# A four-layer graph network on one core: layer 3's product before its aggregation, and all engines reordered

## The chip, the cores and the metric

The kernel runs on one core of a Trainium2 chip. The metric is the device time of one execution in microseconds (us). The kernel before took 2079.52 us, the median of three runs between 2079.24 and 2079.53.

A core has five engines that run their own instruction streams in order and wait for one another by semaphores: TensorE (PE, matrix products into PSUM), VectorE (DVE), ScalarE (ACT), GpSimd (POOL) and SyncE (SP). In this kernel SP issues every DMA.

## The reference

`x` is 128 graphs of 128 nodes by 512 features, `adj` one 128 x 128 matrix of weights shared by all graphs. Four layers follow, each of the form `x = layernorm(x + layer(x))`:

```python
# layer 0: normalized adjacency
nadj = adj * deg**-0.5[:, None] * deg**-0.5[None, :]
y0 = nadj @ (x @ W0) + bias
# layer 1: with W1 = W2 = adj its result is one number per node, the same in all 512 features
# layer 2: attention without softmax
q, k, v = x @ Wq.T, x @ Wk.T, x @ Wv.T
rel = adj.T * (q @ k.T);  rel = rel / norm(rel, axis=2)
y2 = rel @ v
# layer 3: graph attention
h = x @ W
e = leaky_relu((h @ a1)[:, None] + (h @ a2)[None, :]) * adj
y3 = elu(softmax(e) @ h + beta * h)
```

The layernorm behind layer 1 takes its constant away again, so layers 0 and 1 share one layernorm with a changed variance (line 638). The kernel computes layer 3 as elu of (att + beta I) applied to x and W, in one order or the other. It leaves out the -1 of elu, a constant that the layernorm behind it takes away; elu + 1 is max(z, 0) + min(exp(z), 1).

## The kernel before

The 128 graphs are worked in 32 groups of four. All arithmetic is in float32. Each group goes through four large products, named for their weights: **w** (layer 0), **z** (x times Wq^T Wk, made in the head), **v** (layer 2's values) and **k** (layer 3's W). Each is made with one level of Strassen's scheme: seven block products in the order 1, 2, 5, 7, 6, 3, 4 instead of eight, with sums of blocks of the left side (four per group, tile S) and sums of blocks of the weights (made once). A block product is four matmul calls, each of which shows as two instructions in the profile. Product 6 is added in PSUM onto 1's bank, 3 onto 5's and 4 onto 7's.

Nothing is scheduled automatically. The order of the work is written out as a list of steps, `group.step`, in three strings: HEAD, then TURN once for each group from FIRST to the end less LAST (with group numbers shifted by one each time), then TAIL. Each engine's own order follows from this list. The head in the kernel before fills the pipeline with groups 0 to 3 and part of 4; TURN is repeated 21 times. The steps, with their engines:

- `ld`: SP loads x of a group (five tiles of x exist). `y`: PE makes (nadj x)^T, sixteen matmul calls of 128 x 128; `cy`: ACT copies it out; `sy`: POOL makes the sums S.
- `w1` to `w7`: the block products of w. `dw`: DVE adds them onto x; `tw`: ACT copies the 1+6 sum, `uw`: POOL adds that. `bi`: POOL adds the bias.
- `st`, `va`, `po`, `nb`, `ap` with w, v or k: layernorm. DVE takes statistics of each of the four graphs and the variance, POOL its power -1/2, DVE the shift, ACT applies both.
- `xt0` to `xt3`: DVE transposes x in squares of 32 into a tile u, of which there is one; `xd`: SP moves the squares with sixteen DMAs to their places, which completes the transpose; `sx`: POOL makes S.
- `z1` to `z7`, with `cz`, `dz`, `tz`, `uz`: z and its elimination into C_z by ACT, DVE and POOL. `r0` to `r3`: PE multiplies C_z with x transposed, 32 instructions. `rm`: DVE masks; `sq`: ACT takes norms; `rp`: POOL; `rt`: DVE transposes rel in squares; `wr`, `cr`: SP sends it through a DRAM tile and reads it back with four DMAs (`across`).
- `v1` to `v7`, with `cv`, `dv`, `tv`, `uv`: v into C_v. `f0` to `f3`: PE multiplies rel with C_v, one matmul call per graph; `fa`: DVE adds it, times the norm, onto x. 
- `sc`: DVE makes the two scores of each graph for layer 3; `pw`, `pe`: SP sends one through DRAM to all partitions. `pl`, `ej`, `ei`, `ex`, `rd`, `so`: leaky relu, mask, softmax and + beta I on ACT and DVE. `at`, `aw`, `cat`: att is transposed and moved as rel is.
- `h`: PE makes (att x)^T, sixteen matmul calls of 128 x 128 (pv in the profile); `ch`: ACT copies it out; `sh`: DVE makes S out of PSUM. `k1` to `k7`, with `ck`, `dk`, `tk`, `uk`: k into C_k. `ee`, `em`, `ea`: elu out of C_k, in three instructions a block: exp on ACT, max with 0 added onto x on DVE, min with 1 added onto x on DVE. `stk` to `apk`: the last layernorm; `fin`: SP stores a graph.

Line 552 holds the block products, 605 the matmuls of y and h, 691 rel's, 734 f's. Lines 441, 444 and 438 are the helpers of DVE, POOL and ACT. Lines 832, 836 and 840 are elu; 515 is the move of the transposed squares; 525 and 529 are the way through DRAM. Six banks of PSUM rotate among all matmul outputs; two more are held by the score vectors.

In a repeated round of the kernel before PE does w (of one group), h, v, f, k, y, z and r, the last two for the same group and next to each other.

Of the kernel before, what the change touches and what calls it, by code (L numbers as in the profile page):

```python
# [37 lines left out]
F32 = mybir.dt.float32  # L39
# [7 lines left out]
GB = 4  # L47
# [3 lines left out]
FIRST = 4  # L51
LAST = -7
# [4 lines left out]
0.dw7 0.bi00 0.w3 0.tw 0.bi11 1.ld 0.w4 0.bi01 0.uw10 0.dw3 1.y10 0.uw01 1.y00 0.dw4 1.cy10  # L57
1.y11 1.cy00 0.uw11 0.stw0 1.y01 1.cy11 0.stw1 1.sy1 s.g0 1.cy01 0.stw2 1.sy0 0.stw3 0.vaw s.q00
0.pow s.q01 s.g1 s.cg0 0.nbw 1.sy2 0.apw0 0.apw1 0.xt0 1.bi10 2.ld 3.ld 0.apw2 0.xt1 4.ld 1.sy3
0.apw3 0.xt2 s.g2 s.cg1 0.xt3 1.bi00 s.q02 s.q03 s.g3 s.q10 s.cg2 s.q11 s.q12 s.q13 s.bi 1.bi11  # L60
1.w1 0.xd s.cg3 s.s30 s.sg0 1.w2 1.dw1 1.bi01 s.sg2 1.w5 s.sg1 s.sg3 1.w7 1.dw5 1.dw2 s.s32 1.w6
1.dw7 s.s31 1.w3 1.tw s.s33 1.uw01 1.w4 1.uw10 1.dw3 1.stw0 s.t0 1.uw11 s.t1 1.dw4 s.ct0 s.t2
s.ct1 1.stw1 0.sx0 s.t3 s.ct2 0.z1 1.stw2 s.ct3 0.sx1 1.stw3 0.z2 0.cz1 1.vaw 0.sx2 s.sv0 1.pow
0.z5 0.dz2 0.sx3 1.nbw 1.apw0 0.z7 s.sv2 0.cz5 s.sv1 1.apw1 0.z6 0.dz7 1.apw2 1.xt0 1.apw3 s.sv3
0.z3 0.tz 1.xt1 0.uz11 1.xt2 1.xt3 0.z4 0.dz3 1.xd 2.y10 0.dz4 2.y00 2.cy10 2.bi10 2.y11 2.cy00
2.bi00 2.y01 2.cy11 2.sy0 0.r0 2.cy01 0.r1 2.sy1 0.r2 2.sy2 0.r3 0.v1 0.rm 2.bi11 0.rt 0.sq0
0.sq1 2.sy3 0.v2 0.cv1 0.wr 0.sq2 2.bi01 0.sq3 0.v5 0.dv2 0.rp 0.cr 1.sx0 0.v7 0.cv5 1.sx1 0.v6
0.dv7 1.sx2 0.v3 0.tv 1.sx3 0.uv11 0.v4 0.dv3 s.wa 0.dv4 0.f0 0.f1 0.fa0 0.stv0 0.f2 0.fa1 0.f3
0.fa2 3.y10 0.fa3 3.y00 3.cy10 3.bi10 0.stv1 3.y11 3.cy00 0.stv2 3.bi00 3.y01 3.cy11 0.stv3
3.sy0 1.z1 3.cy01 0.vav 0.pov 1.z2 1.cz1 3.sy1 0.nbv 0.apv0 0.apv1 1.z5 0.sc00 3.sy2 0.apv2  # L70
0.sc01 3.bi11 0.apv3 0.sc10 1.z7 1.cz5 0.sc11 3.sy3 0.sc20 1.z6 1.dz7 3.bi01 0.sc21 1.z3 1.tz
0.sc30 1.uz11 0.sc31 1.dz2 1.z4 0.pw 1.dz3 2.w1 1.dz4 2.w2 2.dw1 0.pe 2.w5 2.dw2 2.w7 2.dw5
0.pl0 0.pl1 0.pl2 0.pl3 2.w6 2.dw7 0.ej 0.ei 2.w3 2.tw 0.ex0 2.uw01 0.ex1 2.w4 0.ex2 2.uw10
2.dw3 0.ex3 2.stw0 2.uw11 1.r0 0.rd 2.dw4 1.r1 0.so0 0.so1 1.r2 0.so2 0.so3 2.stw1 1.r3 0.at
1.v1 1.rm 0.aw 2.stw2 1.sq0 1.v2 1.sq1 2.stw3 1.cv1 1.sq2 2.vaw 2.pow 1.sq3 1.v5 1.dv2 0.cat
1.rp 1.rt 2.nbw 2.apw0 1.v7 1.cv5 2.xt0 1.wr 2.apw1 1.v6 1.dv7 2.apw2 2.xt1 2.apw3 2.xt2 1.v3
1.tv 2.xt3 1.cr 1.uv11 1.v4 1.dv3 0.h10 2.xd 1.dv4 0.h00 0.ch10 0.h11 0.ch00 0.sh1 0.h01 0.ch11
0.sh0 1.f0 0.ch01 0.sh2 1.f1 1.fa0 1.f2 0.sh3 1.f3 1.fa1 1.fa2 0.k1 1.fa3 1.stv0 0.k2 0.ck1
1.stv1 1.stv2 0.k5 1.stv3 0.dk2 0.k7 0.ck5 1.vav 0.em00 1.pov 0.ee00 0.ea00 0.k6 0.dk7 2.sx0
1.nbv 1.apv0 2.sx1 0.k3 1.apv1 1.sc00 1.apv2 2.sx2 1.sc01 0.k4 1.apv3 1.sc10 2.sx3 0.tk 1.sc11  # L80
2.z1 1.sc20 0.uk11 1.sc21 1.sc30 0.ee11 2.z2 2.cz1 1.sc31 0.dk3 1.pw 2.z5 2.dz2 0.dk4 2.z7
0.em11 2.cz5 0.em01 0.ea11 2.z6 1.pe 2.dz7 0.ee01 0.em10 2.z3 0.ea01 2.tz 0.stk0 0.ee10 2.uz11
0.stk1 1.pl0 2.z4 1.pl1 2.dz3 1.pl2 1.pl3 0.ea10 2.r0 2.dz4 2.r1 1.ej 2.r2 0.stk2 1.ei 2.r3
0.stk3 1.ex0 2.v1 1.ex1 2.rm 1.ex2 0.vak 2.rt 0.pok 1.ex3 2.v2 2.cv1 2.wr 1.rd 1.so0 2.sq0 1.so1
1.so2 2.sq1 2.v5 1.so3 2.sq2 2.dv2 2.sq3 0.nbk 2.rp 0.apk0 2.v7 2.cr 1.at 2.cv5 0.apk1 2.v6
0.apk2 2.dv7 0.apk3 1.aw 0.fin0 2.v3 2.tv 0.fin1 2.uv11 0.fin2 2.v4 2.dv3 0.fin3 1.cat 2.f0
2.dv4 2.f1 2.fa0 2.stv0 2.f2 5.ld 2.fa1 2.f3 2.fa2 3.w1 2.fa3 2.stv1 3.w2 3.dw1 2.stv2 3.w5
3.dw2 2.stv3 3.w7 2.vav 3.dw5 2.pov 2.nbv 2.apv0 3.w6 3.dw7 2.apv1 2.sc00 2.apv2 2.sc01 3.w3
3.tw 2.sc10 2.apv3 3.uw01 2.sc11 3.w4 2.sc20 3.uw10 3.dw3 1.h10 2.sc21 3.uw11 1.h00 3.dw4 1.ch10
3.stw0 1.h11 1.ch00 3.stw1 1.h01 1.ch11 1.sh1 1.k1 1.ch01 1.sh0 1.sh2 1.k2 1.ck1 3.stw2 1.sh3  # L90
3.stw3 1.k5 2.sc30 3.vaw 2.sc31 1.k7 3.pow 1.ck5 1.dk2 2.pw 3.nbw 1.ee00 1.em00 1.k6 3.apw0
1.dk7 3.apw1 1.ea00 1.k3 3.xt0 3.apw2 3.xt1 3.apw3 2.pe 3.xt2 1.k4 1.tk 3.xt3 1.uk11 1.dk3 3.xd
4.y10 1.dk4 1.ee01 1.em11 4.y00 2.pl0 4.cy10 1.em01 4.y11 4.cy00 1.em10 2.pl1 4.y01 1.ea01
4.cy11 4.sy1 4.w1 1.stk0 2.pl2 4.cy01 1.stk1 2.pl3 4.sy0 1.ee11 4.w2 4.dw1 2.ej 1.ea11 4.w5 2.ei
4.sy2 1.ee10 4.dw2 2.ex0 4.bi10 4.w7 2.ex1 4.dw5 2.ex2 2.ex3 1.ea10 4.w6 4.dw7 4.sy3 2.rd 1.stk2
4.bi00 4.w3 4.tw 2.so0 2.so1 4.w4 2.so2 2.so3 1.stk3 3.sx0 2.at 3.z1 3.sx1 1.vak 2.aw 4.dw3
4.dw4 3.sx2 3.z2 3.cz1 1.pok 3.z5 3.dz2 2.cat 3.sx3 1.nbk 1.apk0 4.bi11 3.z7 3.cz5 1.apk1 1.fin0
4.bi01 1.apk2 1.fin1 3.z6 3.dz7 1.apk3 1.fin2 4.uw10 1.fin3 3.z3 4.uw01 4.uw11 4.stw0 3.z4
4.stw1 6.ld 3.tz 4.stw2 2.h10 3.uz11 3.dz3 2.h00 2.ch10 3.dz4 2.h11 2.ch00 4.stw3 2.h01 2.ch11
2.sh1 3.r0 4.vaw 2.ch01 2.sh0 4.pow 3.r1 2.sh2 4.nbw 3.r2 2.sh3 4.apw0 3.r3 4.apw1 4.xt0 4.apw2  # L100
3.v1 4.xt1 3.rm 4.apw3 4.xt2 3.sq0 3.v2 3.cv1 3.rt 3.sq1 4.xt3 3.wr 3.sq2 3.v5 3.sq3 3.dv2 3.rp
3.v7 3.cv5 3.cr 3.v6 3.dv7 3.v3 3.tv 3.uv11 3.v4 3.dv3 3.f0 4.xd 3.dv4 3.f1 3.fa0 3.stv0 3.f2
3.fa1 3.f3 3.fa2 2.k1 3.fa3 3.stv1 2.k2 2.ck1 3.stv2 3.stv3 2.k5 2.dk2 3.vav 2.ee00 2.em00 3.pov
2.k7 2.ck5 2.ea00 3.nbv 3.apv0 2.k6 2.dk7 3.apv1 3.sc00 3.apv2 3.sc01 2.k3 3.apv3 3.sc10 4.sx0
2.tk 3.sc11 2.k4 4.sx1 3.sc20 3.sc21 4.sx2 5.y10 3.sc30 5.y00 5.cy10 3.sc31 2.uk11 2.dk3 5.y11
3.pw 5.cy00 4.sx3 2.dk4 2.ee11 5.y01 5.cy11 2.em11
"""
TURN = """
4.z1 5.cy01 2.em01 2.em10 4.z2 4.cz1 3.pe 2.ea11 5.sy0 2.ee01 4.z5 4.dz2 5.sy1 4.z7 4.cz5 2.ea01
3.pl0 5.sy2 2.stk0 2.ee10 2.stk1 4.z6 3.pl1 5.bi10 3.pl2 4.dz7 3.pl3 3.ej 4.z3 4.tz 2.ea10 3.ei  # L110
4.uz11 4.z4 4.dz3 3.ex0 5.sy3 3.ex1 2.stk2 3.ex2 4.r0 2.stk3 3.ex3 5.bi00 4.dz4 4.r1 3.rd 5.bi11
2.vak 4.r2 4.r3 3.so0 2.pok 3.so1 5.w1 3.so2 3.so3 4.rm 5.bi01 3.at 4.sq0 5.w2 4.sq1 5.dw1 3.aw
4.sq2 2.nbk 4.sq3 2.apk0 5.w5 4.rp 5.dw2 2.apk1 2.fin0 2.apk2 2.fin1 4.rt 5.w7 2.apk3 3.cat
5.dw5 5.w6 5.dw7 4.wr 5.w3 5.tw 2.fin2 5.uw01 2.fin3 5.w4 5.uw10 5.dw3 4.cr 5.stw0 5.uw11 3.h10
5.dw4 3.h00 5.stw1 3.ch10 3.h11 5.stw2 3.ch00 7.ld 3.h01 5.stw3 3.ch11 3.sh0 4.v1 3.ch01 5.vaw
3.sh1 5.pow 3.sh2 4.v2 4.cv1 5.nbw 3.sh3 5.apw0 5.apw1 5.xt0 4.v5 4.dv2 5.apw2 5.xt1 5.apw3 4.v7
5.xt2 4.cv5 5.xt3 4.v6 4.dv7 4.v3 4.tv 4.uv11 4.v4 4.dv3 4.f0 5.xd 4.dv4 4.f1 4.fa0 4.stv0 4.f2
4.fa1 4.f3 4.fa2 3.k1 4.fa3 4.stv1 3.k2 3.ck1 4.stv2 4.stv3 3.k5 3.dk2 4.vav 3.ee00 3.em00 4.pov
3.k7 3.ck5 3.ea00 4.nbv 4.apv0 3.k6 3.dk7 4.apv1 4.sc00 4.apv2 4.sc01 3.k3 4.apv3 4.sc10 5.sx0
3.tk 4.sc11 3.k4 5.sx1 4.sc20 4.sc21 5.sx2 6.y10 4.sc30 6.y00 6.cy10 4.sc31 3.uk11 3.dk3 6.y11  # L120
4.pw 6.cy00 5.sx3 3.dk4 3.ee11 6.y01 6.cy11 3.em11
"""
TAIL = """
4.z1 5.cy01 2.em01 2.em10 4.z2 4.cz1 3.pe 2.ea11 5.sy0 2.ee01 4.z5 4.dz2 5.sy1 4.z7 4.cz5 2.ea01
3.pl0 5.sy2 2.stk0 2.ee10 2.stk1 4.z6 3.pl1 5.bi10 3.pl2 4.dz7 3.pl3 3.ej 4.z3 4.tz 2.ea10 3.ei
4.uz11 4.z4 4.dz3 3.ex0 5.sy3 3.ex1 2.stk2 3.ex2 4.r0 2.stk3 3.ex3 5.bi00 4.dz4 4.r1 3.rd 5.bi11
2.vak 4.r2 4.r3 3.so0 2.pok 3.so1 5.w1 3.so2 3.so3 4.rm 5.bi01 3.at 4.sq0 5.w2 4.sq1 5.dw1 3.aw
4.sq2 2.nbk 4.sq3 2.apk0 5.w5 4.rp 5.dw2 2.apk1 2.fin0 2.apk2 2.fin1 4.rt 5.w7 2.apk3 3.cat
5.dw5 5.w6 5.dw7 4.wr 5.w3 5.tw 2.fin2 5.uw01 2.fin3 5.w4 5.uw10 5.dw3 4.cr 5.stw0 5.uw11 3.h10
5.dw4 3.h00 5.stw1 3.ch10 3.h11 5.stw2 3.ch00 8.ld 3.h01 5.stw3 3.ch11 3.sh0 4.v1 3.ch01 5.vaw  # L130
3.sh1 5.pow 3.sh2 4.v2 4.cv1 5.nbw 3.sh3 5.apw0 5.apw1 5.xt0 4.v5 4.dv2 5.apw2 5.xt1 5.apw3 4.v7
5.xt2 4.cv5 5.xt3 4.v6 4.dv7 4.v3 4.tv 4.uv11 4.v4 4.dv3 4.f0 5.xd 4.dv4 4.f1 4.fa0 4.stv0 4.f2
4.fa1 4.f3 4.fa2 3.k1 4.fa3 4.stv1 3.k2 3.ck1 4.stv2 4.stv3 3.k5 3.dk2 4.vav 3.ee00 3.em00 4.pov
3.k7 3.ck5 3.ea00 4.nbv 4.apv0 3.k6 3.dk7 4.apv1 4.sc00 4.apv2 4.sc01 3.k3 4.apv3 4.sc10 5.sx0
# [788 lines left out]
```

## Time and profile before

| | before |
|---|---|
| median of three runs | 2079.52 us |
| the profiled execution, its own time | 2078.88 us |
| its span, first to last instruction | 2076.9 us |
| mean granted PE clock | 0.997 |
| DMA packets; of these under 512 B | 364,341; 283,425 |
| one move of transposed squares: 16 issues on SP | 11.54 us |
| relT's and attT's DMAs, 64 KB each, to landing | 2.0 us |
| elu's two DVE passes, mean | 1093 and 1155 ns |
| fa, DVE with one input from PSUM, mean | 697 ns |

The span and the run's time differ by what lies around the first and the last instruction, here 1.98 us. Means come from the groups of instructions by line; the mean of fa is its busy time, 89.2 us, over 128 instructions, since successive instructions overlap a little and the page's mean of one, 739 ns, counts the overlap twice. For PE this matters more: a block matmul shows 379 ns from start to modelled end, but 56 of them take 12.09 us, 216 ns each, since they are pipelined.

A row of waits reads: the waiting engine and what it ran next, what it waited for, the sum in us, how often, the longest. A row of the stretch table reads: the stretch, its length, then the busy time of PE, PE's weight load, DVE, ACT and POOL, the granted PE clock, the DMA share and GB/s.

### The profile page before, as it was taken

The numbers are of one execution on the slowest core, as the hardware profiler recorded it, in microseconds if no ns is written. First come the engines' busy times: TensorE is split into PE (matmuls) and PEld (weight loads), VectorE is DVE, ScalarE is ACT, GpSimd is POOL, SyncE is SP. The second block draws the span as 40 slices with busy tenths as digits, with TensorE's granted clock in tenths as the row PEclk, the third lists the DMA queues.
The fourth block names the chain that finished last, engine by engine and source line by source line (L and its number), as shares of the span: only waits on it lengthen the run. The fifth ranks groups of instructions, "written<-read, shape, count | busy, mean of one in ns | idle before, by whom it ended". The sixth has DMA issues, their size and how long they took to land.

```text
span 2076.9 us, 29797 instructions
## 1 busy us (share of the span) xinstructions
PE 2033.5 (98%) x10554; PEld 1796.7 (87%) x10554; DVE 1605.9 (77%) x3048; ACT 842.0 (41%) x1737; POOL 916.6 (44%) x712
## 2 busy tenths in 40 slices
PE   9999999999999999999999999999999999999996
PEld 6888988888888888888888888888888888888885
DVE  6578788777887778787778877788877878776777
ACT  2333434444443334343343443444343434343345
POOL 5632554434544445443355444454434554436211
PEclk9999999999999999999999999999999999999998
DMA  7222322332223332223322133222233122232212
GB/s 232 39 46 66 91 67 43 86 82 79 74 42 71 82 87 67 62 51 87 82 73 73 36 85 82 80 73 45 68 82 87 66 66 47 77 92 46 47 51 91
DMA packets 364341, 150.74 MB, mean 73 GB/s; under 512 B 283425, under 2 KB 316321, under 8 KB 364193
## 3 DMA queue, kind: packets, MB, share of 16 engines
q1 hardware_dynamic: 364192, 148.84, 28.3%
q8 instruction: 84, 1.38, 0.3%
q14 instruction: 65, 0.52, 0.1%
HBM read 64.82 MB, written 50.40 MB: 55 GB/s over the span
## 4 chain that ended last, share of the span: by engine, by line
PE 78%; DVE 16%; issue 4%; ACT 1%; SPq 1%; POOL 0%; DMA 0%; POOLq 0%; ACTq 0%; DVEq 0%
PE p_v L552 18%; PE p_w L552 18%; PE p_k L552 17%; PE pv L605 5%; PE p_z L552 5%; PE pf L734 5%; DVE x L840 4%; PE pr L691 4%; PE py L605 4%; DVE st_k L631 3%; DVE x L836 3%; DVE C_z L441 2%; DVE C_k L441 1%; ACT ex L832 1%; DVE nmax L790 1%
## 5 line engine op out<-in xcount | busy, mean ns | idle before, releaser
L441 DVE TENSOR_TENSOR x<-p_w,x 128x512 f32<-128x512 f32 x192 | 131.8, 688 | 153.6 <-PE p_w L552 77.7
L444 POOL TENSOR_TENSOR x<-x,t_w 128x512 f32<-128x512 f32 x96 | 119.3, 1271 | 173.2 <-ACT t_w L438 172.8
L753 DVE SCALAR_TENSOR_TENSOR prod<-x,wa_bc 128x512 f32<-128x512 f32 x256 | 175.7, 686 | 22.3 <-ACT x L653 8.7
L444 POOL TENSOR_TENSOR x<-x,bias_bc 128x512 f32<-128x512 f32 x128 | 173.0, 1363 | 14.1 <-PE py L605 13.1
L552 PE MATMUL p_k<-w_t,S_v 128*128 128x256 f32 x768 | 171.2, 379 | 1.6 <-ACT C_k L438 1.6
L552 PE MATMUL p_z<-S_x,gq_t 128*128 128x256 f32 x768 | 171.0, 379 | 0.0
L552 PE MATMUL p_v<-wvT_t,S_x 128*128 128x256 f32 x768 | 171.0, 379 | 0.0
L552 PE MATMUL p_w<-w_t,S_y 128*128 128x256 f32 x768 | 171.0, 379 | 0.0
L448 POOL TENSOR_TENSOR r_v<-v,minus_half 128x4 f32<-128x4 f32 x32 | 43.7, 1366 | 286.8 <-DVE v L640 286.6
L552 PEld LDWEIGHTS p_k<-w_t,S_v 128*128 128x128 f32 x768 | 145.8, 190 | 21.8 <-ACT C_k L438 2.0
L552 PEld LDWEIGHTS p_w<-w_t,S_y 128*128 128x128 f32 x768 | 145.9, 190 | 19.8
L552 PEld LDWEIGHTS p_v<-wvT_t,S_x 128*128 128x128 f32 x768 | 145.9, 190 | 19.8
L552 PEld LDWEIGHTS p_z<-S_x,gq_t 128*128 128x128 f32 x768 | 145.9, 190 | 19.8
L840 DVE SCALAR_TENSOR_TENSOR x<-ex,x 128x512 f32<-128x512 f32 x128 | 147.8, 1155 | 10.1 <-ACT ex L832 5.1
L832 ACT ACTIVATE ex<-C_k 128x512 f32<-128x512 f32 x128 | 80.8, 631 | 147.7 <-DVE x L840 84.4
L836 DVE SCALAR_TENSOR_TENSOR x<-C_k,x 128x512 f32<-128x512 f32 x128 | 135.6, 1093 | 0.0
L441 DVE TENSOR_TENSOR C_v<-p_v,t_v 128x512 f32<-128x512 f32 x64 | 44.3, 692 | 114.0 <-PE p_v L552 114.0
L444 POOL TENSOR_TENSOR C_v<-C_v,t_v 128x512 f32<-128x512 f32 x32 | 40.5, 1265 | 200.9 <-ACT t_v L438 196.0
L438 ACT COPY C_k<-p_k 128x512 f32<-128x512 f32 x64 | 37.2, 585 | 224.1 <-PE p_k L552 224.0
L605 PEld LDWEIGHTS py<-nadjT,x 128*128 128x128 f32 x1024 | 121.9, 196 | 2.7 <-DVE nadjT L372 0.8
L605 PE MATMUL py<-nadjT,x 128*128 128x128 f32 x1024 | 122.3, 279 | 0.4 <-DVE nadjT L372 0.4
L653 ACT ACTIVATE x<-x,nb,r_v 128x512 f32<-128x512 f32 x128 | 94.4, 804 | 68.3 <-DVE nb L647 68.3
(959 smaller groups left out, 4754.8 us busy)
## 6 DMA issues: line engine op xcount, KB each, us to landing
out_dram<-x SPq DMA_DIRECT2D x128, 256.0 KB, 2.3
x<-in_x_dram SPq DMA_DIRECT2D x31, 1024.0 KB, 5.4
d_r<-ru SPq DMA_DIRECT2D x32, 256.0 KB, 2.1
relT<-d_r SPq DMA_DIRECT2D x128, 64.0 KB, 2.0
s<-d_s SPq DMA_DIRECT2D x32, 256.0 KB, 3.9
d_a<-au SPq DMA_DIRECT2D x32, 256.0 KB, 2.0
attT<-d_a SPq DMA_DIRECT2D x128, 64.0 KB, 2.0
x<-in_x_dram SPq DMA_DIRECT2D x2, 512.0 KB, 4.6
```

What stands on the lines that cost most here:

```text
L441: nc.vector.tensor_tensor(o, a, b, f)
L444: nc.gpsimd.tensor_tensor(o, a, b, f)
L552: nc.tensor.matmul(ps[:, j, :], lhsT=lhsT, rhs=rhs, start=(i not in ONTO and j == 0 and kc == 0), stop=(j == 1 and kc == 1), skip_group_ch ...
L605: nc.tensor.matmul(o, lhsT=self.x_chunk(b, kc), rhs=rhs, start=True, stop=True)
L631: nc.vector.bn_stats(st, self.x[:, b, :])
L653: nc.scalar.activation(xt, xt, AF.Identity, bias=self.nb[k][:, b : b + 1], scale=self.rstd[k][:, b : b + 1],)
L691: nc.tensor.matmul(self.pr[:, b, :], lhsT=self.whole["z"][:, fc, b // 2, bass.ts(b % 2, P)], rhs=self.xT.chunk(b, fc), start=(fc == 0), st ...
L734: nc.tensor.matmul(self.pf[b], lhsT=self.relT.rearrange("p q r b -> p b (q r)")[:, b], rhs=self.whole["v"][:, b, :], start=True, stop=True,)
L753: nc.vector.scalar_tensor_tensor(prod, self.x[:, b, :], 1.0, wide(wa_bc[k]), ALU.mult, ALU.mult, accum_out=self.s[:, k, b : b + 1],)
L832: nc.scalar.activation(self.ex[p, h], self.k_block(p, h), AF.Exp)
L836: nc.vector.scalar_tensor_tensor(o, self.k_block(p, h), 0.0, o, ALU.max, ALU.add)
L840: nc.vector.scalar_tensor_tensor(o, self.ex[p, h], 1.0, o, ALU.min, ALU.add)
```

## The change

Layer 3 is turned around. The product with W is made first, out of x transposed, as z and v are; then att + beta I multiplies C_k, one matmul call per graph, as f does with C_v. elu reads its argument from PSUM, and exp writes its result back over it. The steps `h` (16 calls), `ch` and `sh` go. New are `nt` and `nd`, which transpose and move x after the second layernorm as `xt` and `xd` do after the first, through the same tile u, and `sn`, the sums of n on POOL. The x that is transposed there is the one that `sc` reads.

```diff
-                "k": Product(f"k_{g}", self.v, "3"),
+                "k": Product(f"k_{g}", self.nT, "3"),
...
-        def pe_h(self, p, h):
-            self.v.make(p, h, lambda o, b, kc: self.times(o, b, kc, self.attT[:, :, b, :]))
+        def nt(self, b):
+            self.nT.square(b, self.x[:, b, :])
+
+        def nd(self):
+            self.nT.move()
...
+        def left_times(self, k, left, b):
+            ps = psum.tile([P, D], F32, tag="bank", name=f"pl_{k}_{self.g}_{b}")
+            nc.tensor.matmul(ps, lhsT=left[:, b, :], rhs=self.whole[k][:, b, :], start=True, stop=True)
+            return ps
...
-        def ee(self, p, h):
-            self.ex[p, h] = mid.tile([P, 2, HD], F32, tag="ex", name=f"ex_{self.g}_{p}_{h}")
-            nc.scalar.activation(self.ex[p, h], self.k_block(p, h), AF.Exp)
-
-        def em(self, p, h):
-            o = self.x_block(p, h)
-            nc.vector.scalar_tensor_tensor(o, self.k_block(p, h), 0.0, o, ALU.max, ALU.add)
-
-        def ea(self, p, h):
-            o = self.x_block(p, h)
-            nc.vector.scalar_tensor_tensor(o, self.ex[p, h], 1.0, o, ALU.min, ALU.add)
+        def h(self, b):
+            self.pz = self.pz if b else {}
+            self.pz[b] = self.left_times("k", self.attT, b)
+
+        def em(self, b):
+            xt = self.x[:, b, :]
+            nc.vector.scalar_tensor_tensor(xt, self.pz[b], 0.0, xt, ALU.max, ALU.add)
+
+        def ee(self, b):
+            nc.scalar.activation(self.pz[b], self.pz[b], AF.Exp)
+
+        def ea(self, b):
+            xt = self.x[:, b, :]
+            nc.vector.scalar_tensor_tensor(xt, self.pz[b], 1.0, xt, ALU.min, ALU.add)
```

The tiles that carry rel and att across partitions get one layout for both, [graph, 128] in a row, so that f's and h's left sides lie without gaps. The runs of their DMAs become 32 numbers (128 bytes) where they were 128:

```diff
-        d = dram.tile([P, 4, P], F32, tag="sq", name=f"d_{name}")
+        d = dram.tile([P, GB, 4, 32], F32, tag="sq", name=f"d_{name}")
...
-        by_t = d.rearrange("(q i) t x -> t i q x", q=4)
+        by_t = d.rearrange("(q i) b t r -> t i b q r", q=4)
         for t in range(4):
-            nc.sync.dma_start(out=o[rows(t)], in_=by_t[t])
+            nc.sync.dma_start(out=o[rows(t)].rearrange("i b (q r) -> i b q r", q=4), in_=by_t[t])
...
-            self.ru = mid.tile([P, 4, 32, GB], F32, tag="ru", name=f"ru_{self.g}")
...
+        def square(self, name, t):
+            u = mid.tile([P, GB, 4, 32], F32, tag="ru", name=f"{name}_{self.g}")
+            nc.vector.transpose(u, t.rearrange("p b (t a) -> p b t a", t=4))
+            return u
```

All three order strings are new. FIRST goes from 4 to 10 and LAST from -7 to -5, so TURN is repeated 17 times instead of 21. On PE the repeated round is now z, f, r, w, y, v, h, k, where f stands between the z and the r of one group. The new TURN begins and ends so:

```diff
-FIRST = 4
-LAST = -7
+FIRST = 10
+LAST = -5
...
+4.z1 2.dk4 2.ex0 1.fin3 2.ex1 4.sx2 2.ex2 4.z2 4.cz1 4.sx3 2.ex3 2.rd 4.z5 6.ld 4.dz2 2.so0
+2.so1 2.so2 4.z7 4.cz5 2.so3 2.at 2.aw 4.z6 4.dz7 4.z3 4.tz 4.uz11 2.cat 4.z4 4.dz3 3.f0 4.dz4
+3.f1 3.fa0 3.f2 3.stv0 3.f3 3.fa1 3.fa2 4.r0 3.fa3 4.r1 3.stv1 4.r2 3.stv2 4.r3 3.stv3 5.w1 4.rm
+3.vav 4.sq0 4.rt 3.pov 4.sq1 5.w2 5.dw1 4.wr 4.sq2 4.sq3 3.nbv 3.apv0 4.rp 5.w5 5.dw2 3.apv1
+3.nt0 3.apv2 3.sc00 4.cr 5.w7 3.apv3 5.dw5 3.nt1 5.w6 5.dw7 3.nt2 3.nt3 5.w3 5.tw 3.sc01 3.nd
...
+5.vaw 3.sc30 5.pow 3.sc31 4.v5 6.sy2 3.pw 5.nbw 4.dv2 6.sy3 4.v7 5.apw0 4.cv5 6.bi11 5.xt0
+5.apw1 4.v6 4.dv7 5.apw2 3.sn0 3.pe 5.xt1 5.apw3 5.xt2 4.v3 4.tv 3.sn1 5.xt3 3.sn2 4.v4 4.dv3
+3.pl0 3.pl1 4.uv11 3.pl2 2.h0 5.xd 4.dv4 3.pl3 3.sn3 2.h1 2.em0 2.h2 2.ee0 2.em1 6.bi01 2.ea0
+2.h3 2.ee1 2.em2 3.k1 2.em3 2.ee2 2.ea1 2.ee3 3.k2 2.ea2 3.ck1 2.ea3 2.stk0 3.k5 2.stk1 2.stk2
+3.k7 3.ck5 2.stk3 3.ej 3.k6 2.vak 3.dk7 2.pok 3.ei 3.k3 3.tk 2.nbk 3.dk2 2.apk0 3.uk11 2.apk1
+2.fin0 3.k4 3.dk3 5.sx0 2.apk2 2.fin1 2.apk3 2.fin2 5.sx1
```

In HEAD the making of z's weight (Wq^T Wk) and the weight products for the scores move ahead of group 1's first product. In TAIL the last steps of PE are now k and h of groups 29, 30 and 31 in turn, after f of group 31.

## The prediction

> **What bounds the kernel now.** I read the page's busy table first, then the chain of waits around one steady round, then the stretch table, then the wait list.
>
> ```profile
> PE 2033.5 (98%) x10554; PEld 1796.7 (87%) x10554; DVE 1605.9 (77%) x3048; ACT 842.0 (41%) x1737; POOL 916.6 (44%) x712
> ```
>
> TensorE (PE) is busy 98% of the span, so only two things can shorten it: less matmul work, or fewer holes between matmuls. One round of the chain shows both (start, us, what):
>
> ```profile
> 361.93 12.09 PE p_w L552 x56
> 374.02 3.57 PE pv L605 x32
> 377.59 12.09 PE p_v L552 x56
> 389.68 3.45 PE pf L734 x8
> 393.12 12.09 PE p_k L552 x56
> ...
> 410.54 1.75 DVE x L836
> 412.29 1.69 DVE x L840
> ...
> 420.17 0.67 DVE nmax L790
> 420.85 0.60 DVE C_z L441
> ...
> 423.06 0.59 DVE C_z L441
> 423.64 0.04 issue
> 423.69 2.05 PE pr L691 x16
> 425.74 1.30 PE p_w L552 x6
> ```
>
> A product costs PE 12.09 us; pv, py and pr cost 3.57 each, pf 3.45. A round needs 4 x 12.09 + 3 x 3.57 + 3.45 = 62.52 us, but p_w starts at 361.93 and again at 425.74: 63.81. From 298.14 to 1638.39 the chain has 21 rounds, 63.82 each. So **1.30 us a round are lost**, and the chain says where: it leaves PE after py, runs on VectorE (DVE) for some 16 us and returns to PE in the middle of pr. PE had reached rel's product and waited for the last two C_z blocks. Why DVE was behind is in the stretch table (length, busy us of each engine):
>
> ```profile
> 397.70:425.74 28.04, 27.27 (x156) 24.56 (x155) 25.99 (x48) 13.21 (x29) 21.40 (x16) 1.00 0.06 10
> ```
>
> DVE is busy 25.99 of 28.04 us there, POOL 21.40, and in it elu's two DVE passes took up to 1.75 us. How often PE waited:
>
> ```profile
> PE pr L691 <- DVE C_z L441: 17.8, 46, 0.6
> ```
>
> 46 waits are two a round in 23 rounds; 23 x 1.30 = **29.9 us**. The page's PEclk shows 9 tenths or more in every slice but the last, so the clock plays no part.
>
> **The change, part by part**, against the profiled execution (span 2076.9, run 2078.88; the median, 2079.52, lies 0.64 above it).
>
> *PE work.* x times att^T (pv, 3.57 a group) goes; the new h step, four att-times-C_k matmuls of pf's form, comes at pf's 3.45. 32 x 0.12 = -3.8 us. The two pf-like steps get unstrided weights: pf's weight loads take 308 ns against 190 elsewhere, but lie beside 431 ns matmuls, so I count nothing.
>
> *The hole before rel.* In the new repeated order the four f matmuls of another group stand between the last product of z and rel. That is 3.45 us of PE work while DVE writes the last two C_z blocks (0.68 us each, in DVE's order ahead of the first fa). The hole has to go unless DVE is over 3 us late: -29.9. Nor do banks hold f back: six rotate, and its four were last read by dk3, dk4, tz and dz2, all earlier.
>
> *DVE, per group.* Gone: four S sums from pv (0.688) = 2.75, and elu's passes out of SBUF (1.093 and 1.155, four each) = 8.99. New: the same eight passes out of PSUM, four transposes of x (83.4/128 = 0.65) = 2.61, and rel's transpose falls from 1.14 to 0.70. The eight passes are not in the trace; above, their old price, below, the nearest row, fa, which is the same kind of instruction with one PSUM input: 89.2/128 = 0.70. The Trainium skill (SBUF — State Buffer, "SBUF: two separate sides") says a DVE operation with two SBUF inputs and a GpSimd operation that reads SBUF exclude each other for a whole instruction. The rows agree: two SBUF inputs, up to 1.76 us; fa, 0.72 to 0.75. I take 0.70: 5.6 (at the old price DVE would still have 10 us free in the round). Sum -4.0, from 50.5 to 46.5 us in a round of 62.4. The same rule speaks against the change, since POOL gets more to do; yet of large operations with two SBUF inputs only e times adj remains (0.70, not stretched). One POOL instruction of 1.27 in front of each would cost DVE 1.3 us a round, and it has 16 free.
>
> *POOL and ACT.* POOL gets four sums of n (1.27) = 5.1 a group, from about 29 to 34 of 62.4 us. ACT loses four copies of pv (0.585). Exp now goes from PSUM to PSUM, not in the trace; between the copy's 0.585 and the old exp's 0.631, hidden at 41% busy.
>
> *A second transposed x through the same scratch tile and SP.* This is the risky part. n needs 16 more DMAs a group on SP's queue, and u, the tile they read, is single and shared with x's transpose. A round's clock, from the first z product: z to 12.1, f 15.5, r 19.1, w 31.2, y 34.8, v 46.9, h 50.3, k 62.4. After f: the fa/statistics run and rel's mask bring the variance to about 20.2, POOL's power (1.37) 21.6, four normalizations 25.2, and the fourth transpose, behind w's eliminations, 28.4. The move's 16 issues took 11.54 us in the trace, landing 2.3: done at 42.2. Only then may the next x transpose write u. DVE has then reached v7 (41.7), so about half a microsecond is stall there, and dv2 and the first normalization lie just before it. Behind it on DVE wait dv7, which v4 (45.1) needs, then xt1 to xt3. They end near 45.2; x's move lands at 59.0. z1 comes at 62.4: 3.4 us to spare. The first S sum follows POOL's uk11 (60.9) and ends at 62.2; z5 asks for it at 65.9. Also behind n's issues on SP: the broadcast of s, landing near 46 (3.9 after its issue), just when ACT wants it; behind that on ACT waits h's first exp, due at 48.5. Value 0 with a bound of 1 us a round; I put 0.2 x 17 repeated rounds = +3.4.
>
> *Shorter runs.* relT and attT now arrive in 128-byte runs instead of 512. The skill (DMA: Bandwidth & Descriptors, "Specifications") asks for at least 512 B for full rate. The row: moves of x, 64 KB in 128-byte runs, land in 2.3 us; relT's, 64 KB in 512-byte runs, in 2.0. By the row +0.3 us; by the rule, as an estimate with the rate falling as the run, 4 x 2.0 = 8.0. relT now has some 50 us from its write to f, attT some 38 to h, so the sum is 0 either way.
>
> *Head.* g's products move ahead of group 1. x_0's transposes then stand behind eight weight products and the weight sums on DVE and begin near 41 instead of 33; the move starts about 45 and lands 15 us later, as now; PE arrives at 59. Wait 1 us instead of 2.1: -1.1. Little else can stall; +1.
>
> *Tail.* The last k product now ends 3.45 us before PE does. DVE then runs eight elu passes (0.70) and four statistics (0.83); the third and fourth matmul pace the first four, so 9.6 us after the first h to the variance, then 7.45 to the end as now (2069.45 to 2076.9): 14.5 after PE's end, where it was 16.9. -2.4. The 1.6 us wait of p_k for C_k at 2037.3 goes too. Against that, DVE from the last f to the last h: fa and statistics 6.4, k eliminations 8.2, transposes 2.6, scores 6.1, two groups' elu 11.2 and statistics 6.9, attention 6.6, small ones 1.5 = 49.5 us, where PE has 46.6. DVE becomes the bound for these: +3.
>
> Sum: -3.8 -29.9 -1.1 -2.4 -1.6 +3.4 +1 +3 = -31.4; run 2047.5, beside the median 2048.1. **2048 us.**
>
> **Rivals.**
>
> *A. The single tile u and SP decide (slower).* Place: nt, 16 issues, xt, 16 issues, z1. Price: 32 issues of 0.72. For it: the first move took 13.52 us, 0.845 an issue, and single issues up to 1.48. At 0.845 the 3.4 us are used up and 0.6 us a round lost. From 0.88 on, 1.7 us a round in about 20 rounds eats the whole gain; at 0.90 it is 2.4 x 20 = 47: **2095**. Against it: that first move ran beside the input loads; in the steady rounds 11.5 holds.
>
> *B. The hole moves.* h holds four banks through max, exp, min; k5 takes the first of them 3.5 us after h ends, and x's first S sum has 3.7 us. If something new is late in each round, half the hole stays: 20 x 0.65 = **2061**; the whole of it: 2074. For it: DVE is still 75% busy, and elu is now three alternating steps between two engines. Against it: every slack found is over 2 us.
>
> *C. The end is DVE's.* If the 3 us become 13 through waits for exp and the softmax chain: **2058**.
>
> *D. The gain is eaten by B and C together:* about 2079, no change.
>
> **How the numbers follow.** My forecast (2041 to 2056) 0.70, C within it or just above; B 0.20; D 0.04; A 0.06. The bottom is the sum without my three allowances (7.4): 2041. The top takes in C and B's half: 2063, which leaves out nearly all of A and D and B's upper part, under 2 in 10. 0.2%, about 4 us, is what a measurement of this kernel can tell from no change; faster 0.90, same 0.04, slower 0.06.
>
> **What would show it.** Round length by successive p_w near 62.5 (right), 63 or more (B, A); no wait of pr for C_z; elu's passes near 0.70; n's move near 11.5 us of issue with the same landing; waits of z for x's move (A) or of k for elu (B); the last 60 us with PE waiting on DVE by about 3. Wrong altogether if z1 is seen to wait for DMA in each round.

## The result, and the profile after

The changed kernel takes 2047.84 us (median of 4 runs, 2047.48 to 2050.26), the kernel before 2079.38 in the same comparison: a ratio of 0.9851, 95% interval 0.9834 to 0.9868, or 31.5 us less. The forecast was 2048.0. The profiled execution is the longest of the four (2050.26 us, span 2048.5), so its own sum comes out 2.4 us higher than the median's.

The first line is the page's table of busy times (us, share of the span, instructions), the others are the whole list of PE's waits (us in total, times, longest):

```profile
PE 2020.1 (99%) x9786; PEld 1699.6 (83%) x9786; DVE 1472.0 (72%) x3048; ACT 771.8 (38%) x1609; POOL 1006.9 (49%) x840
PE pt_nadj L414 <- DVE nadj L410: 4.6, 1, 4.6
PE pl_k L778 <- DVE C_k L487: 3.0, 1, 3.0
PE pl_v L778 <- DMA relT<-d_r: 2.8, 1, 2.8
PE p_k L595 <- DVE C_k L487: 1.9, 2, 1.1
PE p_k L595 <- DVE x L880: 1.0, 1, 1.0
PE pl_k L778 <- DMA attT<-d_a: 0.8, 1, 0.8
PE py L639 <- DVE nadjT L418: 0.4, 1, 0.4
```

The 46 waits of pr for C_z are gone, and so is the wait for x_0T. What is left lies in the first 60 us (pt_nadj, py) or in the last 80, none of it in a repeated round. The chain of waits around one of these rounds (start, us, what) is PE alone, where before it crossed to DVE for some 16 us:

```profile
726.78 12.09 PE p_w L595 x56
738.87 3.57 PE py L639 x32
742.44 12.09 PE p_v L595 x56
754.53 3.43 PE pl_k L778 x8
757.96 12.09 PE p_k L595 x56
770.05 12.09 PE p_z L595 x56
782.13 3.43 PE pl_v L778 x8
785.57 3.57 PE pr L737 x32
789.14 12.09 PE p_w L595 x56
```

From one p_w to the next are 62.36 us, which is exactly 4 x 12.09 + 2 x 3.57 + 2 x 3.43. It was 63.82. In DVE's timeline of the changed kernel around the end of z (start, us, engine, line, operation; in brackets the idle time before it and what ended it) one sees how early DVE now is:

```profile
402.90 0.69 DVE L487 TENSOR_TENSOR C_z<-p_z,C_z 128x512 f32<-128x512 f32 x1 [1.04 <-PE p_z L595]
406.35 0.69 DVE L487 TENSOR_TENSOR C_z<-p_z,t_z 128x512 f32<-128x512 f32 x1 [2.76 <-PE p_z L595]
408.01 0.69 DVE L487 TENSOR_TENSOR C_z<-p_z,t_z 128x512 f32<-128x512 f32 x1 [0.97 <-PE p_z L595]
```

Each of the last C_z blocks is written as soon as its product ends: DVE stood idle for 2.76 us ahead of the third and 0.97 us ahead of the fourth. Before, DVE had elu's passes, statistics and the softmax maximum in that place and was late. This already raises the question of the experiments: the forecast said that f's place between z and rel closes the hole. Here DVE seems early enough without it.

Behind the head, the one place where PE now waits is the tail. PE's and SP's timelines of the changed kernel:

```profile
1973.53 5.18 PE L778 MATMUL pl_v<-C_v,relT 128*128 128x512 f32 x8 [2.85 <-DMA relT<-d_r]
1954.86 11.74 SPq L558 DMA_DIRECT2D n_30T<-sq_n  x16
1966.69 0.57 SPq L568 DMA_DIRECT2D d_r<-ru  x1
1969.02 2.61 SPq L572 DMA_DIRECT2D relT<-d_r  x4
```

Rel of the last group was ready for its trip through DRAM at 1960.5 (the end of its transpose on DVE). It left at 1966.69, because the 16 issues of n_30's move stood ahead of it on SP's queue. PE waited 2.85 us, and the eight matmuls behind the wait took 5.18 us, where the same eight took 3.60 in the group before. Later PE waits 2.96 us in the middle of group 30's h, and the four matmuls behind that wait take 3.41 us, where the four ahead of it took 1.96. The table of stretches shows why: right behind both waits the granted clock (third number from the end) is half of the 1.00 that the rounds have.

```profile
1973.53:1976.00 2.47, 2.47 (x3) 1.14 (x4) 0.31 (x1) 0.00 (x0) 1.13 (x1) 0.50 0.19 32
2014.61:2016.00 1.39, 1.39 (x2) 0.81 (x3) 1.39 (x4) 0.85 (x5) 0.00 (x0) 0.50 0.00 0
```

### The profile page after: what moved, and what is told of

Read it like the earlier page. It is cut to its first block, busy times and chain, and to the rows that moved or that the text cites. A ratio compares the mean times of both kernels' runs of the same rounds, so it can differ in the third digit from the quotient of the medians.

```text
span 2048.5 us, 29135 instructions
## 1 busy us (share of the span) xinstructions
PE 2020.1 (99%) x9786; PEld 1699.6 (83%) x9786; DVE 1472.0 (72%) x3048; ACT 771.8 (38%) x1609; POOL 1006.9 (49%) x840
## 3 DMA queue, kind: packets, MB, share of 16 engines
q1 hardware_dynamic: 732832, 182.42, 41.2%
## 4 chain that ended last, share of the span: by engine, by line
PE 96%; SPq 1%; DVE 1%; issue 1%; DMA 1%; ACT 0%; POOL 0%; POOLq 0%; ACTq 0%; DVEq 0%
PE p_z L595 19%; PE p_w L595 19%; PE p_v L595 18%; PE p_k L595 17%; PE py L639 6%; PE pl_v L778 5%; PE pr L737 5%; PE pl_k L778 5%; SPq L558 1%; PE pg L425 1%; DVE prod L797 0%; SPq L572 0%; ACT x L699 0%; DMA s<-d_s 0%; DVE C_k L487 0%
## 5 line engine op out<-in xcount | busy, mean ns | idle before, releaser
L595 PE MATMUL p_k<-w_t,S_n 128*128 128x256 f32 x768 | 171.5, 379 | 2.9 <-DVE C_k L487 1.9
L490 POOL TENSOR_TENSOR x<-x,bias_bc 128x512 f32<-128x512 f32 x128 | 162.1, 1278 | 15.6 <-PE py L639 13.7
L595 PEld LDWEIGHTS p_k<-w_t,S_n 128*128 128x128 f32 x768 | 145.7, 190 | 23.8 <-DVE C_k L487 2.7
L753 ACT ACTIVATE sq<-rel 128x128 f32<-128x128 f32 x128 | 39.6, 309 | 267.0 <-DVE rel L487 264.3
L494 POOL TENSOR_TENSOR r_k<-v,minus_half 128x4 f32<-128x4 f32 x32 | 32.5, 1016 | 214.0 <-DVE v L686 211.4
L699 ACT ACTIVATE x<-x,nb,r_w 128x512 f32<-128x512 f32 x128 | 96.9, 808 | 66.8 <-DVE nb L693 62.2
L778 PE MATMUL pl_k<-C_k,attT 128*128 128x512 f32 x256 | 116.8, 599 | 3.7 <-DVE C_k L487 3.0
L778 PE MATMUL pl_v<-C_v,relT 128*128 128x512 f32 x256 | 116.7, 599 | 2.8 <-DMA relT<-d_r 2.8
L490 POOL TENSOR_TENSOR C_z<-C_z,t_z 128x512 f32<-128x512 f32 x32 | 40.6, 1270 | 160.2 <-ACT t_z L484 160.2
L487 DVE TENSOR_TENSOR C_z<-p_z,t_z 128x512 f32<-128x512 f32 x64 | 44.1, 688 | 91.2 <-PE p_z L595 88.2
```

What stands on the lines that cost most here:

```text
L487: nc.vector.tensor_tensor(o, a, b, f)
L490: nc.gpsimd.tensor_tensor(o, a, b, f)
L494: nc.gpsimd.tensor_tensor(r, v, minus_half, ALU.pow)
L595: nc.tensor.matmul(ps[:, j, :], lhsT=lhsT, rhs=rhs, start=(i not in ONTO and j == 0 and kc == 0), stop=(j == 1 and kc == 1), skip_group_ch ...
L699: nc.scalar.activation(xt, xt, AF.Identity, bias=self.nb[k][:, b : b + 1], scale=self.rstd[k][:, b : b + 1],)
L753: nc.scalar.activation(scratch, self.rel[:, b, :], AF.Square, accum_out=self.n2[:, b : b + 1])
```

## The experiments

Each run was timed beside the kernel before, which took 2078.6 to 2079.8 us in these comparisons. Differences to the changed kernel are between medians of different comparisons; each ratio's interval is some 3 us to either side, so a difference of a few us says little by itself. Theory H is the forecast's own: f's place closes the hole.

**Rel first.** In the 17 repeated rounds rel's product goes back to directly behind z:

```diff
-4.z4 4.dz3 3.f0 4.dz4 3.f1 3.fa0 3.f2 3.stv0 3.f3 3.fa1 3.fa2 4.r0 3.fa3 4.r1 ...
+4.z4 4.dz3 4.dz4 4.r0 4.r1 4.r2 4.r3 3.f0 3.f1 3.fa0 3.f2 3.stv0 3.f3 3.fa1 3.fa2 3.fa3 ...
```

> In the 17 repeated rounds rel's product stands directly behind z's last product again, and the four f matmuls follow it. Theory H (the place of f is what closed the hole): PE waits for the last C_z blocks again, the old 1.30 us a round, 17 x 1.30 = +22 us on the changed kernel, about 2070. Rival R (the hole was DVE's lateness, and the shorter elu passes alone cure it): pr waits no more than 0.2 us a round, +0 to +4 us, about 2050.

Measured 2052.95 us (ratio to before 0.9878, 0.9865 to 0.9892), 5.1 more than the changed kernel instead of 22. Its chain of waits, then the row of its weight loads' waits for p_w:

```profile
770.61 12.09 PE p_z L594 x56
782.70 3.57 PE pr L736 x32
786.27 3.44 PE pl_v L777 x8
789.71 12.24 PE p_w L594 x56
PEld p_w L594 <- DVE x L486: 5.0, 17, 0.3
```

pr follows z with no gap, and its list of waits has no entry of pr for C_z. The chain shows 0.16 us a round, in p_w (12.24 or 12.25 instead of 12.09), 2.7 us in 17 rounds: once a round its weight loads wait 0.3 us for a DVE instruction that writes x, a wait that the changed kernel does not have. Another 1.1 us lie in the last groups, where one p_w follows another after 78.35 and 75.38 us instead of 77.89 and 74.72. The rest is in the head and the last 170 us, which this edit leaves as they were. Theory H fell: in the new kernel the place of f is worth 5 us or less, not 22.

**Elu from SBUF, alone and with rel first.** ACT copies each of elu's four products to SBUF, and the three steps of elu work there. Only two buffers had room, so the third copy waits for the first block's last pass; the second block's last pass moves ahead of the fourth block's first one for the same reason.

```diff
         def em(self, b):
+            if FIRST - 2 <= self.g < NG + LAST - 2:
+                pz = self.pz[b]
+                self.pz[b] = mid.tile([P, D], F32, tag=("pz", "prod")[b % 2], name=f"pz_{self.g}_{b}")
+                copy(self.pz[b], pz)
```

> In the 17 repeated rounds ACT copies the four products of elu to SBUF and the eight DVE passes read them there; the order of PE stays. Theory H: the passes go from 0.68 to some 1.1 us (about 3.4 us more DVE work a round, beside PE work), PE still never waits in the rounds, within 2 us of the changed kernel. Rival R (the cheaper passes are what closed the hole): +22 us.

> Both edits of the two runs before at once. Theory H: the same as rel first alone, about +22 us. Rival R: each alone costs little and only both together bring the hole back, +22 us here with 0 to +4 in the two others. If the edits cost independently, the sum of the two.

Measured 2071.82 us (ratio 0.9967, 0.9954 to 0.9979) alone, 24.0 more than the changed kernel, and 2086.26 (1.0037, 1.0024 to 1.0050) with rel first, 38.4 more. The size fits rival R, but the place doesn't. PE's waits in the run with elu alone:

```profile
PE p_k L594 <- DVE C_k L486: 17.6, 19, 1.1
```

There is still no wait of pr. The new hole is in **k**, whose evictions stand on DVE behind elu's passes and statistics: from one p_w to the next are 63.63 us instead of 62.36, 1.27 more, 21.6 us in 17 rounds (the list of waits shows 0.9 a round). The two buffers made a chain of copy, pass, exp and pass that takes longer than the passes themselves. So this run does not tell what PSUM is worth for the hole before rel: it made a hole of its own. It does show the price of a pass. DVE's timeline, and POOL's, in one round of it:

```profile
757.60 1.51 DVE L876 SCALAR_TENSOR_TENSOR x<-pz,x 128x512 f32<-128x512 f32 x1 [0.79 <-ACT pz L483]
760.28 0.69 DVE L876 SCALAR_TENSOR_TENSOR x<-pz,x 128x512 f32<-128x512 f32 x1 [1.17 <-ACT pz L483]
757.28 1.28 POOL L489 TENSOR_TENSOR x<-x,bias_bc 128x512 f32<-128x512 f32 x1
```

The same instruction with two SBUF inputs takes 1.51 us when it starts while POOL runs and 0.69 while POOL is idle; the first one starts inside POOL's 757.28 to 758.56 and ends 0.55 after it. That is what the Trainium skill says (SBUF — State Buffer, "SBUF: two separate sides"): the two exclude each other. In the new order elu lies where POOL is mostly idle, so seven of the eight passes of a round cost 0.69 from SBUF too, the same as the 0.68 from PSUM. The passes were therefore not made long again, and whether long passes alone would bring the hole back stays untested. With both edits 9.3 us more are lost than the two cost apart; PE then also waits for ACT's C_k copies (9.9 us in 13 waits). What joins the two stays open.

**The kernel before, with five DVE instructions in another order.** DVE's timeline of the kernel before around the end of z, which came at 420.9 in this round (left out: two short aggregations, and the softmax maximum at 420.17, which the forecast's chain shows):

```profile
418.49 1.76 DVE L840 SCALAR_TENSOR_TENSOR x<-ex,x 128x512 f32<-128x512 f32 x1
420.77 0.68 DVE L441 TENSOR_TENSOR C_z<-p_z,t_z 128x512 f32<-128x512 f32 x1
421.37 0.68 DVE L631 BATCH_NORM_STATS2 st_k<-x 128x6 f32<-128x512 f32 x1
422.18 0.66 DVE L631 BATCH_NORM_STATS2 st_k<-x 128x6 f32<-128x512 f32 x1
422.97 0.66 DVE L441 TENSOR_TENSOR C_z<-p_z,t_z 128x512 f32<-128x512 f32 x1
```

An elu pass, the softmax maximum and two statistics stand ahead of the last two C_z blocks. If this order alone made the hole, it can be closed without any of the change:

```diff
-... 4.dz7 3.pl3 3.ej 4.z3 4.tz 2.ea10 3.ei 4.uz11 4.z4 4.dz3 3.ex0 5.sy3 3.ex1 2.stk2 3.ex2 4.r0
-2.stk3 3.ex3 5.bi00 4.dz4 4.r1 3.rd ...
+... 4.dz7 3.pl3 3.ej 4.z3 4.tz 3.ei 4.uz11 4.z4 4.dz3 2.ea10 3.ex0 5.sy3 3.ex1 3.ex2 4.r0
+3.ex3 5.bi00 4.dz4 2.stk2 2.stk3 4.r1 3.rd ...
```

> The kernel before, with five instructions of DVE's queue in another order in its 21 repeated rounds: the softmax maximum ahead of the third elu pass, that pass behind the third C_z block, two statistics behind the fourth; PE's, ACT's and POOL's orders stay. Theory D (the hole before rel was DVE's order: elu passes and statistics stood ahead of the last two C_z blocks): the waits of pr for C_z go, up to 21 x 1.30 = 27 us less than before, about 2052. Rival L (DVE is too loaded in that stretch, so the lateness turns up elsewhere in the round): half of it or less, 2066 or more. Rival H (only PE work between z and rel helps): no change, 2079.

Measured 2051.05 us (ratio 0.9862, 0.9849 to 0.9876): 28.7 less than the kernel before in the same comparison, the full 27 of theory D and a little more. Its list of waits has 4 waits of pr left (all after 1600 us, in two rounds of the tail, whose order is the old one), and its chain runs through PE alone:

```profile
PE pr L691 <- DVE C_z L441: 1.5, 4, 0.6
719.77 12.09 PE p_z L552 x56
731.86 3.57 PE pr L691 x32
735.43 12.09 PE p_w L552 x56
```

So **the order of DVE's queue** is enough to close the hole. DVE does as much work as before (1603 us of it in the whole span, 1606 before), only in another order, and elu's passes are as long (up to 1.76 us). The reverse was not run: whether short passes in the old order would have closed it too. The result is within about 3 us of the changed kernel's 2047.84, which two comparisons hardly tell apart.

**DVE made late, with f between and with rel first.** Ten maxima over e, whose results nothing uses, stand between the second and third C_z elimination:

```diff
+        def zz(self):
+            for _ in range(10):
+                nothing = self.small("nothing")
+                nc.vector.tensor_reduce(nothing, self.e, AX.X, ALU.max)
...
-... 4.dz7 4.z3 ...
+... 4.dz7 2.zz 4.z3 ...
```

> The changed kernel with ten more DVE instructions a round (a maximum over e, 0.60 to 0.68 us each, its result unused) between the second and the third C_z elimination of z, in the 17 repeated rounds. DVE is idle 2.76 us there and 0.97 us later, so the last two C_z blocks come about 2.4 us after z's end. Theory K (f's four matmuls between z and rel cover a late DVE up to 3.4 us): PE does not wait for C_z, 0 to +4 us on the changed kernel. Rival N (their place is worth nothing): the same hole as with rel first.

> The same ten DVE instructions with rel directly behind z, as in the first run. Theory K: pr waits for C_z 2.0 to 2.4 us in each of the 17 rounds, +34 to +41 us and the 5 us of rel first alone, about 2085 to 2093. Rival N: no more than the run with f between plus 5 us.

Measured 2048.51 us (ratio 0.9857, 0.9842 to 0.9872) with f between, 0.7 more than the changed kernel, and 2088.40 (1.0047, 1.0034 to 1.0059) with rel first, 40.6 more. DVE's timeline with f between, then PE's list of waits with rel first:

```profile
714.69 6.01 DVE L834 TENSOR_REDUCE nothing<-e 128x4 f32<-128x512 f32 x10
720.62 1.28 DVE L486 TENSOR_TENSOR C_z<-p_z,t_z 128x512 f32<-128x512 f32 x2
```

```profile
PE pr L736 <- DVE C_z L486: 29.9, 17, 1.8
```

z ended at 719.16, the C_z blocks came at 721.9, and PE was with f until 722.59: nothing was lost. With rel first the same lateness is a wait in each of the 17 rounds. A round then takes 64.54 us instead of 62.36. So theory K holds: **f's place is a cover**, worth some 40 us when pr would start on its last blocks 2.2 us after z in each of 17 rounds (721.19 to 723.38 in the round of the run with rel first that begins at 709.10). It can be no longer than f's 3.43 us; lateness beyond some 2 us was not tried. In the changed kernel DVE isn't late, and the cover lies nearly unused.

**Short runs, alone on the kernel before.** Rel's layout of the changed kernel, nothing else:

```diff
-            self.relT = mid.tile([P, 4, 32, GB], F32, tag="relT", name=f"relT_{self.g}")
+            self.relT = mid.tile([P, GB, P], F32, tag="relT", name=f"relT_{self.g}")
+            self.way = short_runs(self.relT, self.ru, f"r_{self.g}")
```

> The kernel before, in which rel alone is laid out as in the changed kernel: its transpose has an unstrided output, relT arrives in 128-byte runs, f's weights are unstrided. By the row: relT lands in 2.3 to 2.6 us instead of 2.0, rel's transpose takes 0.70 instead of 1.14, f's weight loads 190 instead of 308 ns, all beside other work: within 3 us of before. By the rule of at least 512 B: relT some 8 us, still hidden in the rounds, and up to 6 us more where it is waited for in the last rounds, 0 to +6 us.

Measured 2079.01 us, ratio 0.9996 (0.9988 to 1.0004): no difference. Its table of DMA issues has the transfer (KB each, median us to landing), the groups by shape have the weight loads of f (busy, mean ns), and the chain of waits has f:

```profile
relT<-d_r SPq DMA_DIRECT2D x128, 64.0 KB, 2.6
L739 PEld LDWEIGHTS pf<-C_v,relT 128*128 128x128 f32 x256 | 48.4, 190 | 47.4 <-issue 38.3 <-PE p_v L561 6.9 <-PE wa_bc L420 0.2
390.85 3.43 PE pf L739 x8
```

Runs a quarter as long land 0.6 us later (2.6 for 2.0), not four times as late. The weight loads fell from 311 to 190 ns and the transpose from 1141 to 703, beside other work. f itself takes 3.43 us instead of 3.45, too little to see in the time of a run: 0.6 us in 32 groups.

**x's move in 32 issues.** The same bytes, twice as many DMAs of half the size:

```diff
-            self.xT.move()
+            self.xT.move(2)
...
+                    for k in range(parts):
+                        kk = slice(k * KC // parts, (k + 1) * KC // parts)
+                        nc.sync.dma_start(
+                            out=self.aT[rows(to), kk, :, rows(q)], in_=self.u[rows(q), kk, :, to]
+                        )
```

> The changed kernel, in which x's move is issued in 32 DMAs of half the size instead of 16 (n's stays at 16). Theory I (an issue costs SP 0.67 us whatever it carries): 21.4 us of issue instead of 10.7; x's move then lands 8.4 us after z1 wants it, and z1 waits for DMA in every round: 20 rounds x 8.4 = +170 us. Theory W (the issue's price goes with the runs it describes): 0.33 to 0.40 an issue, 10.7 to 12.8 us, inside the 2.3 us to spare: 0 to +3 us.

Measured 2354.78 us (ratio 1.1328, 1.1313 to 1.1344), 307 more than the changed kernel. SP's timeline, then a row of PE's waits and the chain of waits, then the table of stretches (length, busy us of PE, PEld, DVE, ACT and POOL with instructions, granted clock, DMA share, GB/s):

```profile
732.39 21.14 SPq L560 DMA_DIRECT2D x_10T<-sq_x  x32
```

```profile
PE p_z L597 <- DMA x_10T<-sq_x: 6.6, 1, 6.6
752.26 1.93 DMA x_10T<-sq_x
754.19 0.25 issue
754.44 14.64 PE p_z L597 x56
```

```profile
754.00:769.00 15.00, 14.56 (x57) 12.50 (x58) 4.01 (x9) 2.15 (x5) 6.24 (x5) 0.83 0.51 172
```

For these moves the price is per issue: 0.66 us at half the bytes, as at the whole (n's sixteen took 10.70 in the same run), so theory I holds. It is not one price for every DMA: d_r's 256 KB in one DMA took SP 0.33 us here. z waits for x in 26 groups, 175 us in all, which is what theory I counted. The rest of the 307 is other waits (PE is idle 223 us more than in the changed kernel) and slower matmuls (its busy time is 2107.5 us instead of 2020.1): behind the wait of 6.6 us shown here the granted clock is 0.83 over 15 us, and z takes 14.64 us instead of 12.09. This is rival A of the forecast, brought about: its mechanism is real, and its cost is higher than the waits alone.

**The tail's DMA order, and POOL's.** The last two moves of n are issued in four parts each, with the trips of rel, att and s between them; in the second run two POOL instructions (the last C_k block of group 30, the power of group 29) are also put ahead of the last group's four sums of n:

```diff
-7.nd 8.r0 ... 8.wr 7.sc31 ... 6.aw 8.dv4 7.sn2 ...
+7.nd0 7.nd1 8.r0 ... 8.wr 7.nd2 8.cr 7.sc31 ... 6.aw 7.nd3 7.sn0 7.sn1 7.sn2 7.sn3 8.dv4 ...
...
-8.nd 6.h1 ... 7.aw 6.em2 6.ee1 8.pw 6.em3 ... 7.cat ... 8.pe ...
+8.nd0 6.h1 ... 7.aw 8.nd1 7.cat 6.em2 6.ee1 8.pw 8.nd2 8.pe 8.nd3 6.em3 ...
... (second run)
-8.sn0 8.sn1 8.sn2 8.sn3 ... 7.uk11 6.vak ... 6.pok
+7.uk11 6.vak 6.pok 8.sn0 8.sn1 8.sn2 8.sn3 ...
```

> Only the last rounds change: the two last moves of n are issued in four parts each, with relT, attT and s between the parts, so that these no longer stand behind 16 issues. Theory Q (the last PE holes of the changed kernel, 9.5 us of waits and 1.8 us of slower matmuls behind them, come from SP's order): -8 to -13 us, about 2037. Rival V (DVE with 49.5 us of work between the last f and the last h against 46.6 on PE is the bound): no more than -4 us.

> The run with the last rounds' DMA order changed, and POOL's queue there mended: the last C_k block of group 30 and the power of group 29 now stand ahead of the four sums of n of the last group. Theory Q (the 5.1 us wait of pl_k for that C_k block, and the slower matmuls behind it, are all that ate the gain of the earlier relT): -5 to -7 us on the run before it, about 2041. Rival V (DVE's 49.5 us take over): -2 us or less.

The first run measured 2047.39 us (ratio 0.9853, 0.9838 to 0.9868), no gain. The wait for relT was gone, and k of group 30 began 5.7 us earlier (1988.39 for 1994.07); then my own order took it back, since the C_k block now stood on POOL behind sums that waited for the last move:

```profile
PE pl_k L780 <- POOL C_k L488: 5.1, 1, 5.1
```

The second run measured **2041.08 us** (ratio 0.9816, 0.9802 to 0.9829), 6.8 less than the changed kernel and the fastest of all. Its waits of the tail, whole:

```profile
PE p_k L597 <- DVE C_k L485: 2.4, 2, 1.3
PE pl_k L780 <- DVE C_k L485: 1.1, 1, 1.1
PE p_k L597 <- DVE x L882: 1.0, 1, 1.0
```

All that is left, 4.5 us, is PE waiting for DVE.

## Why the prediction was right, and where its reason was not

| step of the sum | forecast | measured, and how |
| --- | --- | --- |
| PE work | -3.8 | -5.1: 62.36 for 62.52 a round, x 32; f and h take 3.43 with unstrided weights, which the forecast put at nothing |
| hole before rel | -29.9 | -29.9: no wait of pr for C_z is left |
| allowance in the rounds (u, SP) | +3.4 | 0: the rounds are exactly the sum of PE's work |
| head | -1.1 + 1 | -2.1: PE idle 5.01 us of the first 60, was 7.11 |
| tail, after PE's end | -2.4 | -3.1: 2034.66 to 2048.5 is 13.8, was 16.9 |
| wait of p_k | -1.6 | -1.6 |
| tail, DVE as the bound | +3 | +12.5: waits of 9.5, and 3.0 for slower matmuls behind two of them |

The measured column sums to -29.3; the spans differ by 28.4, so 0.9 us of this execution are not placed. Two errors of the forecast nearly cancel: PE's work, the rounds, the head and the end came out 7.4 us better, since hardly an allowance was needed, and the holes of the tail 9.5 us worse. That the median lies within 0.2 us of the forecast is luck to that extent.

**The hole before rel: right amount, but closed twice.** The forecast's step was that f's four matmuls stand between z and rel, so the hole "has to go unless DVE is over 3 us late". The cover works as it said (the two runs with a late DVE), and would have taken the old 1.3 us too. But it isn't needed here: without it only 5.1 us come back. The new orders moved elu's passes, the statistics and the softmax maximum away from the end of z into k's stretch, and DVE is idle when the last C_z products end. The forecast had seen that DVE was 25.99 of 28.04 us busy in that stretch before, and read it as load. The reordered kernel before shows that order alone was enough: five instructions, 28.7 us.

**DVE per group.** The eight passes take 0.68 us (forecast 0.70). The reason given, PSUM input, is one of two: beside an idle POOL they take 0.69 from SBUF as well. How much of the 4.2 us saved per group comes from PSUM and how much from the new place in the round was not separated. (At the old price of the passes DVE would have had 12.5 us free by the forecast's own figures, not 10: 62.4 - 46.5 - 3.4.)

**POOL and ACT.** Hidden, as said. Exp from PSUM to PSUM takes 580 ns, below the range given (585 to 631).

**A second transposed x through the same scratch tile and SP.** The clock of the round held: in the round that begins at 395.89 n's fourth transpose ended some 28 us after z's start (forecast 28.4), and x's move landed about 2.3 us ahead of z (forecast 3.4). n's move took 10.70 us and was done 41.2 us after z's start, its landing counted as the forecast counts it (42.2). The forecast's 11.54 was a move with one long issue: the next one before took 10.71 too, and such issues reached 1.81 us in the kernel before, not 1.48. In the changed kernel they make every second move or so 11 to 12.3 us long, and in ten rounds x's first transpose waits up to 1.8 us for a DMA, either n's move or the one issued right behind it. So the stall on u that the forecast expected is there, and it costs nothing: x's move starts rather when v ends and frees the move's target (SP waits for p_v 63.2 us in 25 times). In the forecast the two times nearly coincided. Rival A needed a dearer issue; the run with 32 issues shows that it would have come true from about four more issues in x's move (4 x 0.66 against 2.3).

**Shorter runs.** Nothing, as said; +0.6 us in place of the row's +0.3, far from the 8 us that the estimate from the rule of the Trainium skill gave (DMA: Bandwidth & Descriptors, "Specifications"). The measurement decides: at 64 KB a transfer the rule costs 0.6.

**Rival B** (the hole moves) did not happen in the rounds. **Rival C** (the end is DVE's) named the right place and nearly the size, 13 for 12.5, but not the cause: the step "DVE becomes the bound: +3" left out SP's and POOL's queues in the tail, and the slower clock behind a wait. With these mended, what remains on DVE is 4.5 us, close to the +3. **Rival D** had nothing to rest on.

## What to carry to other kernels

When an engine waits for a queue that is "nearly full", look first at what stands just ahead of the awaited instruction in that queue: moving five instructions behind it gained almost as much as rewriting a layer. A piece of independent work between a product and its user is worth about the lateness that it covers, and little when the producer is early (here 40 us and 5). In the last rounds, where no next group fills the gaps, look at every queue again: moves in many pieces hold up short urgent trips there, and freeing one queue shows the next.

## What the runs showed of the hardware that was not expected

- A long wait costs PE more than its length, and short ones did not. Behind waits of 2.85 and 2.96 us the granted clock was 0.50 for the next stretch, and eight matmuls took 5.18 us instead of 3.60; behind one of 6.6 us it was 0.83 over 15 us, and a product took 14.64 instead of 12.09. The parts of the hole that the kernel before had in each round (0.6 us at most) left it at 1.00, and so did the waits of up to 1.3 us in the tail of the fastest run, whose 24 matmuls behind the longest one took 5.42 us (5.34 elsewhere).
- SP's price of a move of x is per issue: 0.66 us at 32 KB as at 64 KB, with a landing of 2.0 and 2.3 us.
- The list of waits understates a hole. With a late DVE and rel first, pr's waits come to 29.9 us (1.76 a round), but in the chain z ends at 721.19 and pr at 726.77, 2.0 more than pr's own 3.57.
